# A four-layer graph kernel on one Trainium2 core: the last batch's first products of each quarter come together behind the other batches'

## The chip, the cores and the metric

The kernel runs on one core of a Trainium2 chip. The core has five engines that run side by side, each through its own list of instructions in order: TensorE (PE in the profile; its weight loads are shown apart as PEld), VectorE (DVE), ScalarE (ACT), GpSimd (POOL) and SyncE (SP, which here only issues DMAs). They meet through semaphores. The metric is the device time of one execution in microseconds (us), the median of several.

## The reference: what is computed

The input is a batch of 16 graphs with the same adjacency matrix `adj` of 1024 x 1024 nodes and 256 features for each node. There are four layers. Layer 0 scores every pair of nodes and sums over the scored edges:

```python
hidden = relu(pre_u[:, :, None, :] + pre_v[:, None, :, :] + b1)
S = sigmoid(einsum('buvk,ko->buvo', hidden, W2)[..., 0] + b2[0])
a_t = einsum('buv,bud->bvd', S * A_a, h_t)                 # the scored sums
m_t = einsum('uv,bud->bvd', A_m, h_t) * h_t
z_t = beta1 * h_t + beta2 * (a_t @ Wa + ba) + beta3 * (m_t @ Wm + bm)
```

Layer 1 sends messages along `adj` and adds a relu of them. Layers 2 and 3 are attention layers: a projection, a softmax over `leaky_relu(f1_i + f1_j) + adj`, a weighted sum, and the input added.

The change is in the scored sums of layer 0, the line with `a_t`. The kernel multiplies `h_t` by `Wa` first (this product is called `hw`), so the stage computes, for each batch, `hw` transposed times `S * A_a`: a contraction over the 1024 source nodes `u`.

## The kernel before, in words

**Sparse scores, dense products.** `adj` is sparse. The scores are worked out for listed neighbours only, by `score_steps` (L717): GpSimd gathers a row of features for each listed slot (L708), VectorE adds and multiplies (L825, L827), ScalarE sums four batches' results (L831, four instructions for one step), and GpSimd scatters the finished scores into a dense array in HBM, `dense_d` (L713). This work runs beside everything else: a helper (`Side.along`, L888) takes a step from it whenever the main work has advanced by so many us (`PACE`).

**Groups.** The 16 batches are worked on in four groups of four (`GB = 4`). For each group, `with_edges` (L1120) computes the scored sums, and then `group_layers` (L1355) does the other layers. While group g is in its layers, the scores of group g+1 are made. In group 3 no score work is left.

**A quarter.** `with_edges` cuts the 1024 target nodes into four quarters of 256 columns. A quarter holds all eight PSUM banks: one for each of the four batches and two halves of the features, `acc[i][eh]`. Its contraction runs over eight tiles of 128 source nodes, `ut`. For each tile:

- SP loads `gd`, the dense scores of the tile for four batches, 512 KB (`load_gd`, L904; four buffers);
- ScalarE copies it into `gc`, with the batches side by side instead of interleaved (L1129; two buffers, `gc_pool`, L702);
- TensorE makes eight products (L131, the line of the helper `product`), for batch 0 to 3 and both halves: `hw[i]` of the tile times `gc` of that batch, summed in the bank of `acc[i][eh]`.

After the eighth tile, VectorE evicts the eight banks in the order of the batches, adds a bias and what is already in `z` (L1152), and the next quarter takes the same banks. There are 16 quarters in the program, 64 products in each.

**What sets the order.** A scheduling layer decides each engine's list and puts in the waits for data and buffers. So a `gc` copy waits until the products that read its buffer two tiles before are done, until its `gd` has landed, and behind all that stands before it on ScalarE. On top of that the kernel paces itself: `paced(ins, n)` (L123) makes an instruction wait for the product that was issued n products earlier in the program's text. A `gc` copy is paced 16 products back, a `gd` load 24, a score step's L825 six. The list `recent`, which is counted in, follows the order in which `product` is called.

**Around the stage.** Before a group's first quarter the banks belong to the last attention layer of the group before: ScalarE copies them (L1325), VectorE finishes (L1326, L1328), and ScalarE issues the output's DMAs (L1002). After the last quarter come the layer-1 products.

Of the kernel before, what the change touches and what calls it, by code (L numbers as in the profile page):

```python
# [17 lines left out]
P = 128  # L18

GB = 4  # L20
# [50 lines left out]
def gnn_stack_kernel(  # L71
# [29 lines left out]
    NT = N // P  # L101
# [4 lines left out]
    QN = HN // 2  # L106
# [6 lines left out]
    def bank():  # L113
        return psum[-1].tile([P, HN], F32, tag="bank", name="bank")
# [8 lines left out]
    def paced(ins, back=6):  # L123


        if recent:
            after(tc, ins, [recent[max(0, len(recent) - back)]], mybir.DependencyClass.Sync, "keeps pace")
        return ins

    def product(*args, **kw):  # L130
        recent.append(nc.tensor.matmul(*args, **kw))  # L131
        del recent[:-BACK]
        return recent[-1]
# [554 lines left out]
    with tc.If(listed > 0) as arm:  # L688
        with ExitStack() as stack:
# [214 lines left out]
            def load_gd(g, v, ut, **pace):  # L904
                view = dense[g % BUFS][:DUMP].rearrange("(t p v) b -> t p v b", p=P, v=N)
                gd = gd_pool.tile([P, QN, GB], F32, tag="gd", name="gd")
                ins = nc.sync.dma_start(gd, view[ut][:, v * QN : (v + 1) * QN, :])
                put[g].before(paced(ins, **pace))
                return gd
# [207 lines left out]
            def exponential(jt):  # L1117
                paced(nc.scalar.activation(ea[:, jt, :], ea[:, jt, :], AF.Exp), 16)

            def with_edges(g, hw, z):  # L1120

                doing[0] = "edges"
                for v in range(N // QN):
                    cols = slice(v * QN, (v + 1) * QN)
                    acc = [[bank() for _ in range(DH)] for _ in range(GB)]
                    for ut in range(NT):
                        gd = first_gd.pop(0) if first_gd else load_gd(g, v, ut, back=BACK)
                        gc = gc_pool.tile([P, GB, QN], F32, tag="gc", name="gc")
                        paced(nc.scalar.activation(gc, gd.rearrange("p n i -> p i n"), AF.Copy), 16)  # L1129
                        for i in range(GB):  # L1130
                            for eh in range(DH):
                                product(
                                    acc[i][eh][:, :QN], hw[i][:, ut, eh * P : (eh + 1) * P], gc[:, i, :],
                                    start=ut == 0, stop=ut == NT - 1,
                                )
                        if z_loads and ut % 2 == 0:
                            load, i = z_loads.pop(0)
                            paced(load(i), 12)
                        if (to_load or to_exp) and ut % 2 and v:
                            if v > 1 and to_exp:  # L1140
                                exponential(to_exp.pop(0))
                            if to_load:
                                jt = to_load.pop(0)
                                paced(nc.sync.dma_start(ea[:, jt, :], adjT_d[jt]), 16)
                                to_exp.append(jt)
                        yield 3.4 if g or v else 1
                    if v == N // QN - 1:
                        while to_exp:
                            exponential(to_exp.pop(0))
                    for i in range(GB):  # L1150
                        for eh in range(DH):
                            nc.vector.scalar_tensor_tensor(  # L1152
                                z[i][:, eh, cols], acc[i][eh][:, :QN], zbias[:, eh : eh + 1], z[i][:, eh, cols],
                                ALU.add, ALU.add,
                            )
# [264 lines left out]
            for g in range(NGR):  # L1420
                hw, z = loaded.pop(0)
                while g not in finished:
                    next(side.steps)
                side.along(with_edges(g, hw, z))
                if g < NGR - 1:
                    side.along(group_layers(g, z))
                else:
                    for _ in far_ahead(z[2:], pair_layers(g * GB, z[:2], layer_one(z[:2]))):
                        pass
                    for _ in pair_layers(g * GB + 2, z[2:], from_lists(z[2:], msg)):  # L1430
                        pass
# [131 lines left out]
```

## Time and profile before

| | us |
|---|---|
| median of three runs | 3143.56 (3133.77 to 3150.67) |
| the profiled execution, its own time | 3123.2 |
| its span, first to last instruction | 3121.5 |
| TensorE busy | 3074.8 |
| VectorE, ScalarE, GpSimd busy | 2352.6, 1945.1, 1878.9 |
| scored sums, groups 0 to 3 | 121.4, 116.6, 120.0, 110.8 |

The mean granted clock of TensorE is 0.998 of full speed. All durations below are from the one profiled execution, whose time lies 20 us under the median of the runs.

How to read the rows: a row of a timeline has the start (us from the span's start), the duration, the engine, the line of the source, the operation, what it writes `<-` what it reads, the shape, and in brackets how long the engine stood idle before it and what ended that. Rows of equal instructions in sequence are merged (`x2`). A row of waits has who waited, `<-` for what, then the total in us, how many times, and the longest. An fp32 product stands in the profile as two matmul records. Idle time of an engine counts only if the end of the run hangs on it.

### The profile page before, as it was taken

To read this page: it belongs to the slowest core of one execution; us is meant where nothing else is said; L and a number is where in the kernel's file an instruction comes from. 1 tells how busy PE (TensorE), PEld (TensorE's weight loads), DVE (VectorE), ACT (ScalarE), POOL (GpSimd) and SP (SyncE) were. 2 spreads that over 40 slices of the span, in tenths; PEclk is the share of its full clock that TensorE was granted. 3 is DMA by queue.
4 is the path that set the end of the run, shared out by engine and by line. 5 is a ranking of instruction groups with operands and counts; after the bars stand their busy time and mean duration, and the time that the engine had idled before them with its cause. 6 is when DMAs were issued, how large, how long until landed. Compare 5 with 4: busy or idle time off the path is not lost. (4 is left out here: it accounts for less than half of the span.)

```text
span 3121.5 us, 39024 instructions
## 1 busy us (share of the span) xinstructions
PE 3074.8 (99%) x11954; PEld 2179.2 (70%) x11954; DVE 2352.6 (75%) x3183; ACT 1945.1 (62%) x6520; POOL 1878.9 (60%) x1483
## 2 busy tenths in 40 slices
PE   9999999999999999999999999999999999999999
PEld 5544555545547756888875688888568888858888
DVE  7887777768774678999667899966789982157844
ACT  3345565656667876787887677788667764414242
POOL 1156787777664577777666776766777770076600
PEclk9999999999999999999999999999999999999999
DMA  9998898888889776568877665887765565485500
GB/s 321 331 331 310 270 313 260 273 242 253 254 290 331 229 214 202 156 185 285 285 233 207 209 165 171 266 284 232 219 206 164 159 207 166 132 262 156 164 2 28
DMA packets 288420, 699.96 MB, mean 224 GB/s; under 512 B 46141, under 2 KB 141178, under 8 KB 281034
## 3 DMA queue, kind: packets, MB, share of 16 engines
q0 software_dynamic: 128224, 387.80, 42.5%
q1 hardware_dynamic: 132538, 258.46, 23.7%
q10 hardware_dynamic: 27440, 51.13, 4.3%
q8 instruction: 96, 1.57, 0.2%
q14 instruction: 122, 1.00, 0.1%
HBM read 565.83 MB, written 131.41 MB: 223 GB/s over the span
## 5 line engine op out<-in xcount | busy, mean ns | idle before, releaser
L831 ACT ACTIVATE z<-z 128x256 f32<-128x256 f32 x2432 | 979.0, 406 | 574.1 <-DVE z L827 549.0
L825 DVE TENSOR_TENSOR z<-z,u 128x1024 f32<-128x1024 f32 x608 | 738.9, 1220 | 374.8 <-PE bank L131 262.4
L131 PE MATMUL bank<-feats,m 128*128 128x257 f32 x4096 | 909.0, 380 | 0.7 <-ACT st L1325 0.5
L708 POOL DMA_INDIRECT z<-v_d,slot_v x512 | 662.2, 1293 | 376.0 <-ACT z L831 208.1
L131 PEld LDWEIGHTS bank<-feats,m 128*128 128x128 f32 x4096 | 769.4, 190 | 111.2 <-ACT st L1325 1.3
L713 POOL DMA_INDIRECT dense_d<-gt,slot_at x512 | 674.5, 1317 | 184.4 <-issue 130.3
L827 DVE SCALAR_TENSOR_TENSOR z<-z,w2r 128x1024 f32<-128x1024 f32 x608 | 737.3, 1219 | 9.0
L131 PE MATMUL bank<-gc,hw 128*128 128x256 f32 x2048 | 451.8, 382 | 15.6 <-ACT gc L1129 10.5
L831 ACT ACTIVATION_READ_ACCUMULATOR z<-z 128x1 f32 x2432 | 461.6, 190 | 0.0
L131 PE MATMUL bank<-adj_sb,h 128*128 128x512 f32 x1024 | 442.3, 592 | 3.3 <-ACT st L333 2.0
L131 PEld LDWEIGHTS bank<-gc,hw 128*128 128x128 f32 x2048 | 386.6, 190 | 80.2 <-ACT gc L1129 20.7
L1099 DVE SCALAR_TENSOR_TENSOR m<-rho,tau,adj_sb 128x512 f32<-128x512 f32 x512 | 375.8, 742 | 65.6 <-PE bank L131 62.7
L131 PE MATMUL bank<-adjT_in,y 128*128 128x512 f32 (+1 forms) x960 | 403.4, 581 | 6.0 <-DMA adjT_in<-adjT_d 5.9
L131 PEld LDWEIGHTS bank<-adj_sb,h 128*128 128x128 f32 x1024 | 194.3, 190 | 242.7 <-issue 237.5
L131 PEld LDWEIGHTS bank<-adjT_in,y 128*128 128x128 f32 x960 | 182.0, 191 | 221.0 <-issue 203.8
L131 PE MATMUL bank<-w,hT 128*128 128x512 f32 (+1 forms) x1024 | 334.9, 487 | 0.0
L1129 ACT ACTIVATE gc<-gd 128x1024 f32<-128x1024 f32 x128 | 264.7, 2069 | 88.4 <-PE bank L131 74.9
L131 PEld LDWEIGHTS bank<-w,hT 128*128 128x128 f32 x1024 | 194.8, 191 | 141.5 <-issue 118.4
L131 PE MATMUL bank<-g_wT,z 128*128 128x257 f32 x1024 | 231.4, 380 | 1.6 <-ACT st L1325 1.1
L131 PEld LDWEIGHTS bank<-g_wT,z 128*128 128x128 f32 x1024 | 191.8, 190 | 33.2 <-issue 3.1
L708 POOL DMA_INDIRECT z<-v_d,x_node x96 | 124.2, 1294 | 128.6 <-ACT z L831 96.6
L1152 DVE SCALAR_TENSOR_TENSOR z<-bank,zbias,z 128x256 f32<-128x256 f32 x128 | 54.6, 480 | 111.7 <-PE bank L131 111.4
(168 smaller groups left out, 2379.4 us busy)
## 6 DMA issues: line engine op xcount, KB each, us to landing
gd<-dense_d SPq DMA_DIRECT2D x128, 512.0 KB
dense_d<-zero ACTq DMA_DIRECT2D x64, 512.0 KB
adjT_in<-adjT_d SPq DMA_DIRECT2D x112, 256.0 KB
h<-in_x_dram SPq DMA_DIRECT2D x19, 1024.0 KB
u_d<-st SPq DMA_DIRECT2D x64, 256.0 KB
v_d<-st SPq DMA_DIRECT2D x64, 256.0 KB
hw_d<-st SPq DMA_DIRECT2D x64, 256.0 KB
u<-u_d POOLq DMA_DIRECT2D x32, 512.0 KB
```

The source lines that it names most:

```text
L131: recent.append(nc.tensor.matmul(*args, **kw))
L708: return nc.gpsimd.indirect_dma_start(out=dst, out_offset=None, in_=src[:], in_offset=bass.IndirectOffsetOnAxis(ap=at, axis=0), **how,)
L713: return nc.gpsimd.indirect_dma_start(out=dst[:], out_offset=bass.IndirectOffsetOnAxis(ap=at, axis=0), in_=src, in_offset=None,)
L825: paced(nc.vector.tensor_tensor(z, z, u, ALU.add))
L827: nc.vector.scalar_tensor_tensor(zk, zk, 0.0, w2r[:, None, :].to_broadcast([P, GB, D]), ALU.max, ALU.mult)
L831: nc.scalar.activation(zk[:, c, :], zk[:, c, :], AF.Copy, accum_out=s[:, k, c : c + 1])
L1099: nc.vector.scalar_tensor_tensor(m, r[:, cols], ta[:, kt : kt + 1], ea[:, kt, cols], ALU.max, ALU.mult)
L1129: paced(nc.scalar.activation(gc, gd.rearrange("p n i -> p i n"), AF.Copy), 16)
L1152: nc.vector.scalar_tensor_tensor(z[i][:, eh, cols], acc[i][eh][:, :QN], zbias[:, eh : eh + 1], z[i][:, eh, cols], ALU.add, ALU.add,)
```

## The change

Within a quarter, the products of the last batch (`i = GB - 1`, banks 6 and 7) for tiles 0 and 1 are held back. Tile 0 issues the six products of batches 0 to 2. Tile 1 issues its own six, and then the held four: the last batch's two of tile 0, and its two of tile 1. From tile 2 on the order is as before. No product, copy or eviction is added or left out; the buffers' numbers stay.

```diff
                     acc = [[bank() for _ in range(DH)] for _ in range(GB)]
+                    held_back = []
                     for ut in range(NT):
                         gd = first_gd.pop(0) if first_gd else load_gd(g, v, ut, back=BACK)
                         gc = gc_pool.tile([P, GB, QN], F32, tag="gc", name="gc")
                         paced(nc.scalar.activation(gc, gd.rearrange("p n i -> p i n"), AF.Copy), 16)
-                        for i in range(GB):
+
+                        turns = [(ut, gc, i) for i in range(GB - 1 if ut < 2 else GB)]
+                        if ut < 2:
+                            held_back.append((ut, gc, GB - 1))
+                        if ut == 1:
+                            turns += held_back
+                        for kt, scores, i in turns:
                             for eh in range(DH):
                                 product(
-                                    acc[i][eh][:, :QN], hw[i][:, ut, eh * P : (eh + 1) * P], gc[:, i, :],
-                                    start=ut == 0, stop=ut == NT - 1,
+                                    acc[i][eh][:, :QN], hw[i][:, kt, eh * P : (eh + 1) * P], scores[:, i, :],
+                                    start=kt == 0, stop=kt == NT - 1,
                                 )
```

In the changed kernel the lines behind the change stand seven lower: the `gc` copy is L1130, the evictions L1159, and L1325, L1326 and L1328 become L1332, L1333 and L1335.

## The prediction

> **What bounds the kernel now.** I read the page first, then TensorE's waits, then the stage that the change touches, by its four stretches, and last the ScalarE rows inside it.
>
> ```profile
> span 3121.5 us, 39024 instructions
> PE 3074.8 (99%) x11954; PEld 2179.2 (70%) x11954; DVE 2352.6 (75%) x3183; ACT 1945.1 (62%) x6520; POOL 1878.9 (60%) x1483
> ...
> PE bank L131 <- ACT gc L1129: 10.5, 12, 2.2
> ```
>
> TensorE is busy for all but 46.7 us of the span, so a pause put into it lengthens the run, unless a pause already there becomes shorter. The longest named wait is for the `gc` copies of the stage in question (10.5 us in 12 waits). The next view cuts that stage into its four groups (window, its length, then busy time by engine, granted clock, DMA share, GB/s):
>
> ```profile
> 942.00:1063.40 121.40, 114.31 (x517) 96.61 (x516) 64.01 (x80) 103.78 (x210) 52.51 (x45) 1.00 0.88 305
> 1495.40:1612.00 116.60, 113.75 (x517) 96.69 (x516) 75.70 (x96) 106.03 (x246) 69.37 (x58) 1.00 0.84 270
> 2045.30:2165.30 120.00, 114.35 (x516) 97.84 (x515) 77.65 (x92) 105.00 (x243) 74.73 (x62) 0.99 0.84 271
> 2598.00:2708.80 110.80, 110.80 (x516) 97.55 (x515) 15.02 (x37) 61.79 (x31) 0.53 (x1) 1.00 0.47 150
> ```
>
> Group 3 has no score work beside it, and TensorE never pauses: 512 matmul records in 110.8 us are 0.216 us each. An fp32 product is two records, so 0.432 us; a tile of 8 products 3.45; a quarter 27.7. Groups 0 to 2 take 10.6, 5.8 and 9.2 us more (25.6 in all): there ScalarE is busy for some 105 us. Call the copies of a quarter gc0 to gc7. Group 3, around a quarter's start:
>
> ```profile
> 2622.47 2.08 ACT L1129 ACTIVATE gc<-gd 128x1024 f32<-128x1024 f32 x1 [1.40 <-PE bank L131]
> 2625.92 2.06 ACT L1129 ACTIVATE gc<-gd 128x1024 f32<-128x1024 f32 x1 [1.38 <-PE bank L131]
> 2629.37 2.05 ACT L1129 ACTIVATE gc<-gd 128x1024 f32<-128x1024 f32 x1 [1.39 <-PE bank L131]
> 2632.83 2.05 ACT L1129 ACTIVATE gc<-gd 128x1024 f32<-128x1024 f32 x1 [1.40 <-PE bank L131]
> ```
>
> These are gc0 to gc3. There are two `gc` tiles, so gc2 cannot start before the products of gc0 are done: ScalarE idles 1.4 us until TensorE frees a tile, copies for 2.05, and is done ahead of need. gc2 starts at 2629.37, 0.25 after the record that follows gc0's last product (2629.12). It ends at 2631.42; TensorE wants it when tile 1 is done, 0.25 before gc3's start: 2632.58. Slack 1.16 us.
>
> **The change, part by part.** *Work.* The same 64 products per quarter, copies and evictions: 0 us. In the order of the changed program, every quarter runs six products of tile 0, six of tile 1, then the last batch's two of tile 0 as the 13th and 14th, and its two of tile 1. (In groups 1 and 2, whose starts were already permuted, one or two products differ.)
>
> *What it gives: banks 6 and 7 are wanted later.* They are the last that VectorE evicts from the quarter before. The gain is at most what TensorE waits for these evictions: the source view of L1152 gives 0.4 us in two waits of weight loads over the whole run. I take 0.
>
> *What it costs: gc2.* gc0 is now read until the 14th product instead of the 8th, so gc2 starts 6 x 0.432 = 2.59 us later. The slack covers 1.16 less the hand-over from copy to matmul, 0.05 (a copy that ends at 958.18 is followed at 958.23, rows below). The pause is 2.59 - 1.11 = 1.48, and the record after a pause steps 0.32 instead of 0.216: about 1.6 us for each quarter. gc3 then runs straight behind gc2, ends 2.05 after it, 1.4 before it is wanted; the usual spacing is back. Group 3: 4 x 1.6 = 6.4.
>
> *gc1* is wanted after six products (2.59 us into the quarter, was 3.45). In group 3 it ends at 0.25 + 2.06 = 2.31: no wait. Where score work stands ahead of it it ends later: at 3.54 in three quarters (a pause of 1.0), at 3.04 and 2.73 in two (0.5 and 0.2); this also pushes the 14th product.
>
> *Score work queued beside gc2.* In the changed order of eight quarters, the four L831 of one score step (1.6 us; a score batch, below) have moved from behind gc2 to ahead of it. They fill time that ScalarE would have idled, or overrun it. Second quarter of group 1, before:
>
> ```profile
> 1527.53 2.10 ACT L1129 ACTIVATE gc<-gd 128x1024 f32<-128x1024 f32 x1 [0.26 <-ACT gc L1129]
> ...
> 1531.13 2.11 ACT L1129 ACTIVATE gc<-gd 128x1024 f32<-128x1024 f32 x1
> ...
> 1531.20 1.23 DVE L827 SCALAR_TENSOR_TENSOR z<-z,w2r 128x1024 f32<-128x1024 f32 x1
> ```
>
> The quarter starts at 1527.32. Now gc1 ends at 1529.6, a first batch at 1531.2; the second waits for the L827 that ends at 1532.43 and ends at 1534.1; the 14th product is done at 1533.36. So gc2 runs 1534.2 to 1536.3 and tile 2 starts at 1536.35 instead of 1534.33: +2.0. The same working, from each quarter's own rows: first quarters of groups 0 and 1 below; the other three of group 0 +1.0, +0.85, +1.9; of group 1 +2.0, +2.0, +2.3; of group 2 +2.2, +1.4, +1.9. Where it is under 1.5 (between 0.4 and 1.5 for the first of them), a later pause of the old quarter (up to 1.3 us, for a copy or a `gd` load) shrinks by the rest.
>
> *First quarters.* Group 0: tile 2 is 1.5 late, but TensorE already pauses at tiles 4 and 5 for `gd`; the load for tile 4 is paced behind the ninth product, whose time stays, so it lands as before. Between 0 and 1.6, as the load for tile 5 is issued that much later or lands with the backlog: I take the middle, 0.8. Group 1: gc2 starts 7.5 us in already, behind score work and an output DMA, past the new release (6.8): 0. Group 2 is worse. The score step after tile 0 is paced six products back, now the quarter's first product instead of its third, and in the changed VectorE order its L825 comes ahead of the pair of L1328 that frees the sixth bank:
>
> ```profile
> 2048.14 0.87 DVE L1328 SCALAR_TENSOR_TENSOR st<-st,share,bank 128x256 f32<-128x256 f32 x2
> 2052.09 1.23 DVE L825 TENSOR_TENSOR z<-z,u 128x1024 f32<-128x1024 f32 x1 [3.08 <-PE bank L131]
> ```
>
> That L825 waits for its gather, which lands at 2052.00. The pair then runs at 2053.3 to 2054.2 and TensorE, after seven products from 2045.31, stands from 2048.3 to 2054.3. Such a pause costs clock as well: the granted clock after the present one, 2.80 us at 2055.71, was
>
> ```profile
> 2055.70:2059.00 3.30, 3.29 (x8) 0.54 0.90 294
> 2059.00:2080.00 21.00, 21.00 (x98) 0.99 0.91 304
> ```
>
> so the next four products take 0.85 each, the 14th is done at 2059.1, gc2 ends at 2061.4 and tile 2 starts then instead of 2059.04: +2.4.
>
> *Queues.* GpSimd issues one `u` gather two scatters earlier, in group 0; SP moves an `adjT_in` load past a store and the first `gd`; both stay ahead of their users: 0. The `gd` loads from tile 5 on are paced 24 products back and shift with TensorE.
>
> Sum: 6.4 + 3.75 + 6.3 + 5.5 + 0.8 + 0 + 2.4 = 25.15, say 25 us. On the profiled execution (3123.2 us) that is 3148; that execution lies 20 us below the median of the three runs, 3143.56, so against the median I forecast 3169, +0.8%.
>
> **A rule against the trace.** A pause of TensorE that ended in full clock is this one:
>
> ```profile
> 956.16 2.02 ACT L1129 ACTIVATE gc<-gd 128x1024 f32<-128x1024 f32 x1 [3.27 <-PE bank L131]
> 958.23 3.72 PE L131 MATMUL bank<-gc,hw 128*128 128x256 f32 x16 [2.18 <-ACT gc L1129]
> ```
>
> 2.18 us idle cost no clock here, 2.80 did. My pauses of 1.3 to 2.1 idle lie below both, the one of 6 us above. A tripped clock adds 1.7 us (eight records at 0.427 instead of 0.216). Pauses with one score batch more, 1.6 longer (B below), would be of 2.9 to 3.7 and trip it by the row: in eight quarters 13.6 us more. The Trainium skill, "TensorE: Matmul & The Clock Gate", Part 1, says that the clock halves after an idle window of about 3.4 us, counted by a free-running clock; by it most of these pauses would cost no clock, and the sum there would lack those 13.6. For my forecast row and rule give the same, and the measured 2.80 decides where they part.
>
> **The rivals.** *A, swallowed.* Groups 0 to 2 already lose 25.6 us to late copies and loads; if the new pauses only stand in their place, group 3's 6.4 remain, with what exceeds them: about +10, 3153. For: ScalarE is busy for 105 of 120 us there. Against: 15 of the lost us lie in the three first quarters, and in five of the nine others the old pauses after tile 2 sum to under 0.8.
>
> *B, larger.* A second score batch ahead of gc2 in eight quarters (8 x 1.6 = 13), or the clock tripped in as many (13.6): +38, 3182; both, +52. For: batches wait for VectorE (549 us of ScalarE's waits). Against: the order has one more, not two.
>
> *C, the other side: late banks are the real loss at a quarter's start.* From quarter start to tile 2, the 16 quarters lose 11.2 us against 6.91 each, 9.5 of them at the starts of groups 1 and 2, where banks come from L1325 and L1328. If all came back and gc2 were not late, 3132. It decides only where gc2's delay stays under 0.7 us a quarter; against it stand group 3's rows. By this alone the gain stays within 0.5%; run spread would have to add to it.
>
> *D, no change.* A scheduler could restore the old order; the changed program shows the move in all 16 quarters.
>
> **How the numbers follow.** Forecast (+17 to +33) 0.58, A 0.14, B 0.18, C 0.09, D 0.01. The bounds: A's +10 less half of the runs' spread (8) gives 3146, B's +38 with the same gives 3190; I give 3148 to 3190, and 3160 to 3177 for the forecast alone. Within 0.5% (15.7 us) is about what a measurement of this kernel cannot tell from no change. Slower takes the forecast, B and a fifth of A: 0.79. Same: the rest of A, half of C, D: 0.16. Faster: the other half of C, with the spread: 0.05.
>
> **What would show it.** In group 3: gc2 starts 6.3 us into each quarter instead of 3.7, ScalarE idles 4.0 us before it and 0 before gc3, TensorE pauses once a quarter at tile 2 for about 1.3 us of shown idle, and the stretch is 117 us instead of 110.8. In all, `gc` waits go from 10.5 us to some 25 to 30. At the start of group 2, a pause of about 6 us and a half clock after it. Wrong would be: gc2 starting at 3.7 all the same; tile 2 late but the stretches of groups 0 to 2 unchanged (A); pauses over 3 us at tile 2 (B).

## The result and the profile after

| | before | after |
|---|---|---|
| median of six runs each, same chip | 3142.06 (3132.87 to 3150.67) | 3165.61 (3154.68 to 3171.13) |
| ratio of the two, 95% interval | | 1.0079 (1.006 to 1.0098) |
| the profiled execution, its own time | 3123.2 | 3169.96 |

The medians differ by 23.5 us (a ratio of 1.0075); by the interval the change costs between 19 and 31. The page of the changed kernel, with the lines that answer to those of before (a group of instructions has busy time and mean ns of one, then the idle time just before them and what ended most of it):

```profile
span 3168.2 us, 39029 instructions
...
PE 3081.3 (97%) x11954; PEld 2179.1 (69%) x11954; DVE 2352.2 (74%) x3183; ACT 1946.2 (61%) x6520; POOL 1876.7 (59%) x1483
...
L131 PE MATMUL bank<-gc,hw 128*128 128x256 f32 x2048 | 455.2, 382 | 39.1 <-ACT gc L1130 29.4
...
L1130 ACT ACTIVATE gc<-gd 128x1024 f32<-128x1024 f32 x128 | 262.7, 2061 | 109.7 <-PE bank L131 75.3
```

The engines do the same work: ScalarE is busy for 1946.2 us (1945.1 before), the 128 copies take 2061 ns each. TensorE's idle time ahead of the stage's products is what grew: 39.1 us, of which 29.4 are waits for `gc`. Before, the same row had 15.6 and 10.5:

```profile
L131 PE MATMUL bank<-gc,hw 128*128 128x256 f32 x2048 | 451.8, 382 | 15.6 <-ACT gc L1129 10.5
```

TensorE's waits after the change (total in us, times, longest):

```profile
PE bank L131 <- ACT gc L1130: 29.4, 26, 1.7
...
PE bank L131 <- DVE st L1335: 6.2, 1, 6.2
```

The second line is a single pause, at the start of group 2. The stage by its four groups (window, its length, then busy time by engine, granted clock, DMA share, GB/s):

```profile
951.70:1077.80 126.10, 114.56 (x515) 96.19 (x514) 63.70 (x79) 103.58 (x210) 50.95 (x44) 1.00 0.87 294
1509.90:1632.50 122.60, 114.28 (x516) 96.14 (x515) 75.54 (x96) 106.11 (x246) 66.59 (x58) 1.00 0.81 257
2066.60:2196.00 129.40, 115.28 (x516) 97.50 (x515) 77.80 (x92) 104.83 (x243) 72.03 (x62) 0.97 0.78 250
2637.40:2754.40 117.00, 111.87 (x517) 97.22 (x515) 15.02 (x37) 61.29 (x31) 0.53 (x1) 1.00 0.42 142
```

They were 121.4, 116.6, 120.0 and 110.8, so the four take 26.3 us more. In group 3, which has no score work, the reason is in plain sight. A quarter's start there, with ScalarE's copies and TensorE's products (a row has the start, the duration, and in brackets the idle time before it and what ended that):

```profile
2659.70 13.98 PE L131 MATMUL bank<-gc,hw 128*128 128x256 f32 x64
...
2663.41 2.08 ACT L1130 ACTIVATE gc<-gd 128x1024 f32<-128x1024 f32 x1 [1.40 <-PE bank L131]
2666.86 2.07 ACT L1130 ACTIVATE gc<-gd 128x1024 f32<-128x1024 f32 x1 [1.38 <-PE bank L131]
2672.90 3.95 ACT L1130 ACTIVATE gc<-gd 128x1024 f32<-128x1024 f32 x2 [3.98 <-PE bank L131]
...
2674.97 7.39 PE L131 MATMUL bank<-gc,hw 128*128 128x256 f32 x33 [1.29 <-ACT gc L1130]
```

The quarter starts at 2666.61 (this moment and the lengths of single quarters below are read from the matmul records one by one). gc1 starts 0.25 us later. gc2 (the first of the two merged in the row at 2672.90) starts 6.29 us into the quarter instead of 3.7, since its buffer is now read until the 14th product; ScalarE stands idle for 3.98 us before it, and gc3 follows without a gap. TensorE pauses 1.29 us for it, once in every quarter.

The profiled pair differs by 46.7 us, though, and the medians by 23.5. Of the 46.7, the four groups hold 26.9, counted from first to last record of each. The rest lies outside: 9.7 us ahead of the first changed product, 8.6 in the layers of group 2, and so on. The profiled execution of the changed kernel lies near the top of its runs, the other under all of the six of the kernel before. A second profile of each kernel (below) shows what these are.

### The profile page after: what moved, and what is told of

Its sections match the earlier page's. It is cut to its first block, busy times and chain, and to the rows that moved or that the text cites. A ratio compares the mean times of both kernels' runs of the same rounds, so it can differ in the third digit from the quotient of the medians.

```text
span 3168.2 us, 39029 instructions
## 1 busy us (share of the span) xinstructions
PE 3081.3 (97%) x11954; PEld 2179.1 (69%) x11954; DVE 2352.2 (74%) x3183; ACT 1946.2 (61%) x6520; POOL 1876.7 (59%) x1483
## 5 line engine op out<-in xcount | busy, mean ns | idle before, releaser
L825 DVE TENSOR_TENSOR z<-z,u 128x1024 f32<-128x1024 f32 x608 | 738.3, 1219 | 410.2 <-PE bank L131 250.4
L713 POOL DMA_INDIRECT dense_d<-gt,slot_at x512 | 663.6, 1296 | 188.3 <-issue 137.3
L131 PE MATMUL bank<-gc,hw 128*128 128x256 f32 x2048 | 455.2, 382 | 39.1 <-ACT gc L1130 29.4
L1130 ACT ACTIVATE gc<-gd 128x1024 f32<-128x1024 f32 x128 | 262.7, 2061 | 109.7 <-PE bank L131 75.3
L1159 DVE SCALAR_TENSOR_TENSOR z<-bank,zbias,z 128x256 f32<-128x256 f32 x128 | 54.6, 479 | 117.4 <-PE bank L131 117.2
```

The lines of the kernel that those rows point to most:

```text
L713: return nc.gpsimd.indirect_dma_start(out=dst[:], out_offset=bass.IndirectOffsetOnAxis(ap=at, axis=0), in_=src, in_offset=None,)
L825: paced(nc.vector.tensor_tensor(z, z, u, ALU.add))
L1159: nc.vector.scalar_tensor_tensor(z[i][:, eh, cols], acc[i][eh][:, :QN], zbias[:, eh : eh + 1], z[i][:, eh, cols], ALU.add, ALU.add,)
```

## The experiments

Four chips took part; a ratio is always against runs of the kernel before on the same chip. This table puts the profiles side by side. "13 quarters" is the sum of all quarters but the first ones of groups 0, 1 and 2, which stand alone in the last column. A quarter is counted from the start of its first record to the end of its last; a pause between two quarters is in neither (2.8 us behind the 30.32 of the first split, at most 0.9 elsewhere).

| kernel | ratio (95%) | `gc` waits | group 3 | 13 quarters | first quarters of groups 0, 1, 2 |
|---|---|---|---|---|---|
| before | 1 | 10.5 | 110.67 | 369.8 | 31.94, 31.95, 34.77 |
| before, second profile | | 18.7 | 110.67 | 370.9 | 32.84, 37.53, 40.51 |
| after | 1.0079 (1.006 to 1.0098) | 29.4 | 116.87 | 391.5 | 32.81, 32.08, 38.80 |
| after, second profile | | 28.8 | 116.87 | 391.0 | 33.02, 31.70, 41.38 |
| after, copy split 3+1 | 0.9968 (0.9951 to 0.9984) | 10.8 | 110.67 | 369.3 | 31.70, 30.60, 30.32 |
| before, copy split 3+1 | 0.9976 (0.996 to 0.9991) | 8.7 | 110.67 | 370.0 | 32.58, 30.18, 29.32 |
| the same, another chip | 1.0000 (0.9987 to 1.0013) | 8.4 | 110.67 | 369.4 | 31.30, 30.18, 34.36 |
| before, copy split 2+2 | 0.9978 (0.996 to 0.9996) | 6.9 | 110.67 | 370.4 | 30.73, 32.69, 32.70 |
| tile 0's pair after one batch | 0.9994 (0.9977 to 1.0012) | 16.9 | 110.67 | 374.5 | 31.89, 31.61, 38.29 |
| tile 0's pair after two batches | 1.0034 (1.0017 to 1.0051) | 25.0 | 113.51 | 384.0 | 36.33, 31.46, 41.07 |
| first quarters left alone | 1.0071 (1.0046 to 1.0096) | 30.5 | 115.36 | 389.9 | 31.84, 38.63, 31.92 |
| pace restored | 1.0089 (1.0065 to 1.0113) | 34.6 | 116.91 | 392.2 | 32.97, 38.53, 33.87 |
| pace restored, second profile | | 34.3 | 116.89 | 390.7 | 32.41, 37.78, 36.91 |
| before, with the pace alone | 1.0008 (0.9996 to 1.002) | 8.5 | 110.67 | 369.6 | 32.65, 30.81, 31.08 |

### The buffer's release: the copy split, in the changed kernel and in the one before

The theory: the loss is the late release of gc0's buffer. If the last batch, whose products are late, has a tile of its own, the other three batches' buffer is free early again. The order of the products stays.

```diff
-                        gc = gc_pool.tile([P, GB, QN], F32, tag="gc", name="gc")
-                        paced(nc.scalar.activation(gc, gd.rearrange("p n i -> p i n"), AF.Copy), 16)
+                        gc = gc_pool.tile([P, GB - 1, QN], F32, tag="gc", name="gc")
+                        gl = gc_pool.tile([P, 1, QN], F32, tag="gl", name="gl")
+                        by_batch = gd.rearrange("p n i -> p i n")
+                        paced(nc.scalar.activation(gc, by_batch[:, : GB - 1, :], AF.Copy), 16)
+                        paced(nc.scalar.activation(gl, by_batch[:, GB - 1 :, :], AF.Copy), 16)
...
```

In the changed kernel:

> The changed kernel with each gc tile split in two tiles of two buffers each: batches 0 to 2, and the last batch alone (two copies for a tile instead of one, 256 more ScalarE instructions' halves in all). The held products then keep only the small tile. Release theory (the copy of tile 2 waits for the held products of tile 0): the large copy of tile 2 is free after the sixth product, so the pause at tile 2 goes; group 3's stage takes 110.7 us instead of the changed kernel's 116.9, groups 0 and 1 lose 4 to 6 us each, and only the 6 us pause at the start of group 2 stays: about the split control plus 4 to 7 us, 3146 to 3152. Rival, order (TensorE itself pays for the new order of products or banks): group 3 stays near 116.9 and the time near 3165.

In the kernel before, as the control for what the split does by itself:

> The kernel before with the same split of the copies, as a control for what the split costs by itself: one more ScalarE start for each of 128 tiles, some 0.2 to 0.4 us each. Where ScalarE idles (group 3) it is hidden: 110.7 us. In groups 0 to 2 it may add 0 to 3 us each. Total within 0 to +8 us of the kernel before (3142 to 3150), under both theories.

Group 3 of the changed kernel with the split copy (window as above, then some of its copies):

```profile
2603.70:2714.50 110.80, 110.80 (x516) 97.58 (x515) 15.02 (x36) 64.69 (x61) 0.53 (x1) 1.00 0.49 150
```

```profile
2634.26 1.59 ACT L1132 ACTIVATE gc<-gd 128x768 f32<-128x768 f32 x1 [1.30 <-issue]
2636.85 1.59 ACT L1132 ACTIVATE gc<-gd 128x768 f32<-128x768 f32 x1 [1.00 <-PE bank L131]
2638.34 1.20 ACT L1133 ACTIVATE gl<-gd 128x256 f32<-128x256 f32 x2
```

All 110.80 us are busy again, with the products in the changed order. The quarter shown starts at 2631.42; the larger part of gc2 starts at 2634.26, 2.84 us into it instead of 6.29. The 13 quarters take 369.3 us, as in the kernel before. So the order of the products costs nothing by itself; what costs is that one late reader holds a tile of four batches. The Trainium skill, "Perfetto Trace Analysis", Optimizing Scalar/DVE Operations, says that where ScalarE is not saturated but causes bubbles on another engine, breaking up its instructions may let work complete sooner. The split does that here, mainly because it divides the tile and so lets the next copy start sooner. The rows show its price: 1601 + 658 ns for the two parts instead of 2061 for one, some 25 us of ScalarE over the run, of which the 13 quarters show nothing.

Both split kernels are 10 us faster than the kernel before on this chip, which I had not expected. Nor is the changed kernel with the split 4 to 7 us above its control, as forecast: the medians are 3129.89 and 3129.91, and the pause at the start of group 2, forecast at 6 us, was 1.59 in its profile. I come back to it with the third split.

### The dose: tile 0's pair a little earlier

If the release is the cause, the cost must follow it in steps: with tile 0's held products after the first batch of tile 1 the buffer is free two products late, which the slack covers; after the second batch, four products late.

```diff
                         if ut == 1:
-                            turns += held_back
+                            turns = turns[:1] + held_back[:1] + turns[1:] + held_back[1:]
```

> The changed kernel with tile 0's two held products issued after the first batch of tile 1 (as 9th and 10th product instead of 13th and 14th); tile 1's two stay last. Release theory: gc2 is released 2 products later than before, 0.86 us, less than the 1.11 us of slack, so group 3 shows no pause at tile 2 (110.7 us), groups 0 and 1 stand within 2 to 3 us of before, and the pause at the start of group 2 (VectorE's order) stays: 3146 to 3152. Rival, order: the products still change places, so each quarter still pays some 1.5 us: about 3165, group 3 near 117.

The same with `turns[:2]` and `turns[2:]`:

> The same with tile 0's two held products after the second batch of tile 1 (11th and 12th). Release theory: gc2 is released 4 products later, 1.73 us, less 1.11 of slack: a pause of 0.62 us and 0.10 for the record after it, so 0.7 us a quarter; group 3 takes 113.6 us, between 110.7 and 116.9, and the total is about 3153 to 3159. Rival, order: as the changed kernel, 3165, group 3 near 117.

Group 3 after one batch (TensorE, then ScalarE's gc2 and gc3):

```profile
2631.65 13.54 PE L131 MATMUL bank<-gc,hw 128*128 128x256 f32 x62
...
2636.86 2.05 ACT L1130 ACTIVATE gc<-gd 128x1024 f32<-128x1024 f32 x1 [2.25 <-PE bank L131]
2639.45 2.06 ACT L1130 ACTIVATE gc<-gd 128x1024 f32<-128x1024 f32 x1 [0.54 <-PE bank L131]
```

and after two:

```profile
2663.65 3.97 ACT L1130 ACTIVATE gc<-gd 128x1024 f32<-128x1024 f32 x2 [3.12 <-PE bank L131]
...
2665.74 6.53 PE L131 MATMUL bank<-gc,hw 128*128 128x256 f32 x29 [0.45 <-ACT gc L1130]
```

ScalarE's idle time before gc2 goes 1.4, 2.25, 3.12, 3.98 for a release none, two, four and six products late: 0.86 a step, two products. TensorE's pause goes 0, 0, 0.45, 1.29: nothing up to the slack, then one for one. Group 3 takes 110.67, 110.67, 113.51, 116.87. The ratios follow: 0.9994, 1.0034, 1.0079. Only the total of the first missed: 3 us under the kernel before on this chip, where the expectation's 3146 to 3152 was 4 to 10 above the 3142 known then.

### Which quarters: the first ones left alone

```diff
-                        turns = [(ut, gc, i) for i in range(GB - 1 if ut < 2 else GB)]
-                        if ut < 2:
+                        turns = [(ut, gc, i) for i in range(GB - 1 if v and ut < 2 else GB)]
+                        if v and ut < 2:
```

> The changed kernel, but a group's first quarter keeps the order of before (products are held back in quarters 1 to 3 alone). Release theory: the twelve other quarters keep their pause (1.1 to 2.3 us each), the four first ones lose theirs: group 3 takes 110.7 + 3 x 1.56 = 115.4 us, and the first quarters of groups 0, 1 and 2 return to about 31.9, 32.0 and 34.8 us; total 5 to 8 us under the changed kernel, 3158 to 3161. If VectorE's order at the start of group 2 were not tied to the move, that quarter would stay near 38.8.

Group 3, its first quarter and its second (window and length, then busy time by engine):

```profile
2620.50:2648.40 27.90, 27.90 (x132) 24.59 (x131) 4.48 (x12) 14.66 (x8) 0.00 (x0) 1.00 0.57 189
2648.40:2677.70 29.30, 28.00 (x131) 24.32 (x130) 3.62 (x10) 16.30 (x9) 0.00 (x0) 1.00 0.41 144
```

The cost is local: the quarter with the old order takes 27.8 us and never pauses, the next one pauses 1.3. Group 2's first quarter fell to 31.92. But group 1's took 38.63, although its products stand in the old order. That was open here. The 5 to 8 us that the whole run should have gained do not show either: 1.0071 (1.0046 to 1.0096) against 1.0079.

### The start of group 2: the pace of the score step

The prediction put a pause of 6 us down to one L825 that the pace moves ahead of a pair of evictions. It was there (PE and DVE rows of the changed kernel):

```profile
2066.65 3.19 PE L131 MATMUL bank<-gc,hw 128*128 128x256 f32 x14
...
2073.85 1.23 DVE L825 TENSOR_TENSOR z<-z,u 128x1024 f32<-128x1024 f32 x1 [4.07 <-DMA z<-v_d,slot_v]
2075.00 0.87 DVE L1335 SCALAR_TENSOR_TENSOR st<-st,share,bank 128x256 f32<-128x256 f32 x2
...
2076.01 5.63 PE L131 MATMUL bank<-gc,hw 128*128 128x256 f32 x18 [6.17 <-DVE st L1335]
```

The gather landed 7.2 us into the quarter; TensorE stood for 6.17 us behind the pair, and then ran 18 records in 5.63 us, with the clock halved for a part of them. Two kernels take this apart. In the first, the changed order keeps the old pace: two entries more are counted after tile 0, and taken out again at tile 1.

```diff
+                        if ut == 1:
+                            del recent[-2:]
                         turns = [(ut, gc, i) for i in range(GB - 1 if ut < 2 else GB)]
...
+                        if ut == 0:
+                            recent.extend(recent[-1:] * 2)
```

> The changed kernel with the pace of the score step after tile 0 put back: the list that the pace counts in is padded by two, so the step's L825 waits for the third product of the quarter instead of the first. In the built order L825 then stands behind the pair of evictions again at the start of groups 1 and 2; the products are all held back as in the changed kernel. Theory (the extra pause at the start of group 2 comes from L825 ahead of the pair on VectorE, not from the held products): the pause of 6.2 us there falls to about 1.5 and 3 us at the two banks that come late, tile 2 starts some 13.2 us into the quarter instead of 16.3, and the quarter takes 35 to 36 us instead of 38.8; the pauses at tile 2 of the other quarters stay, group 3 takes 116.9; total 2 to 4 us under the changed kernel, 3162. Rival (the pause there belongs to the held products and the release of gc): the quarter stays near 38.8.

The pair ran first and the 6 us pause was gone:

```profile
2068.34 2.32 PE L131 MATMUL bank<-gc,hw 128*128 128x256 f32 x10
2072.74 5.38 PE L131 MATMUL bank<-gc,hw 128*128 128x256 f32 x16 [2.08 <-DVE st L1339]
```

The quarter took 33.87 us, a little under the expectation. Yet the ratio, 1.0089, is no lower than the changed kernel's, and the first quarter of group 1 was again at 38.53. In the second, the kernel before keeps its products and gets the new pace alone. On VectorE this moves one thing at two places: at the starts of groups 1 and 2, an L825 goes ahead of a pair that frees a bank.

```diff
+                        if ut == 1:
+                            recent.extend(skipped)
                         for i in range(GB):
...
+                        if ut == 0:
+                            skipped = recent[-2:]
+                            del recent[-2:]
```

> The kernel before, its products in their old order; only the score step behind tile 0 of each quarter is paced two products further back, as the change does it. On VectorE this moves one thing at two places: at the starts of groups 1 and 2, an L825 now stands ahead of a pair that frees a bank, as in the changed kernel. Theory (the pause at the sixth bank of group 2 comes from that L825, which waits for its gather): a pause at the 11th or 15th record of group 2's first quarter of 2.5 to 7 us, followed by half clock, quarter 37 to 43 us instead of 34.8 and 40.5; all other quarters as before, group 3 110.67, gc waits 9 to 19 us; time 1.000 to 1.003 of the kernel before. Rival (the pause belongs to the late release of gc, or to nothing but the execution): no pause above 2.1 us at the sixth bank, quarter 32 to 41, ratio 0.999 to 1.001. A ratio over 1.004 would say that the pace costs more than the order of the products.

```profile
2042.66 3.19 PE L131 MATMUL bank<-gc,hw 128*128 128x256 f32 x14
...
2045.62 1.23 DVE L825 TENSOR_TENSOR z<-z,u 128x1024 f32<-128x1024 f32 x1 [0.48 <-DMA z<-v_d,slot_v]
2046.76 0.87 DVE L1333 SCALAR_TENSOR_TENSOR st<-st,share,bank 128x256 f32<-128x256 f32 x2
...
2047.78 4.12 PE L131 MATMUL bank<-gc,hw 128*128 128x256 f32 x18 [1.93 <-DVE st L1333]
```

My expectation of a pause of 2.5 to 7 us missed. The chain is the same, gather, L825, pair, TensorE, but the gather landed 3 us into the quarter instead of 7.2, and TensorE stood for 1.93 us. The quarter took 31.08 us, and the ratio says that the pace alone costs between -1 and 6 us. By the expectation's own signs this run fits the rival as well.

All the profiles together decide it. In six of the fourteen the L825 stands ahead of the pair (after and its second profile, after with the split, both dose runs, the pace alone). It starts 7.20, 6.51, 2.62, 3.12, 6.35 and 2.96 us into the quarter, and TensorE's pause ahead of the 15th record is 6.17, 5.47, 1.59, 2.09, 5.32 and 1.93 us: 1.03 or 1.04 less, each time. In the other eight the pair runs first; they pause 0.8 to 2.1 us ahead of the 11th record, where the six do not pause. So the order on VectorE does make TensorE wait for a gather, and the length of that pause is set by when the gather lands. That changes from execution to execution. What the whole quarter loses by it is not shown, as the old order has pauses of its own there.

### What comes back: second profiles of three kernels

The kernel before, unchanged:

> The kernel before, profiled once more. What belongs to the kernel should come back within 1 us: group 3 at 110.7 us, its quarters at 27.79, tile 2 at 6.91 us into a clean quarter, and about 9 to 13 us in waits for gc copies. If a first quarter of group 1 or 2 that took 38 us in other runs (a late landing of a gather or of a gd load) is a matter of the execution, it may turn up here too, in a kernel without the change; if it belongs to the changed order, the first quarters of groups 1 and 2 stay at 30 to 35 us.

The changed kernel, unchanged:

> The changed kernel, profiled once more. My theory: group 3 is again 116.9 us, a clean quarter 29.35 with tile 2 at 8.3 us, and the quarters 2 to 4 of groups 0 to 2 again 29.9 to 31.2; those nine lie 1.1 to 2.3 above the kernel before. The first quarter of group 2 has again a pause before the sixth bank is evicted, but of a length set by when the gather lands: between 1.5 and 7 us, quarter between 33 and 39. The rival, that the excess of the profiled pair outside the stage (9.7 us ahead of the first changed product and 8.6 in the layers of group 2) belongs to the change: then the first changed product starts again at 951.8 +-1 us from the start and the layers behind group 2 take again 8 us more than in the kernel before. By my theory these move by several us from run to run.

The changed kernel with the old pace, once more:

> The changed kernel with the score step's pace restored in the quarters' first tiles, profiled once more. Group 3 again 116.9 us, the first quarter of group 2 again at 33 to 35 us with the evicting pair ahead of the L825. Open is the first quarter of group 1, which took 38.5 us in the profile of this kernel: if that belongs to this kernel's order it comes back within 1 us; if it is a late landing of a gd load in that execution, it is 30 to 33 us here.

The first profile of these three shows the kernel before at the start of group 1:

```profile
1527.29 2.01 ACT L1129 ACTIVATE gc<-gd 128x1024 f32<-128x1024 f32 x1 [5.02 <-remote]
...
1529.35 15.97 PE L131 MATMUL bank<-gc,hw 128*128 128x256 f32 x64 [6.47 <-ACT gc L1129]
```

So the first quarter of 37 to 39 us in group 1 needs no part of the change. It is there in the kernel before, where gc2 waited 5.02 us. `remote` in the row means that the profile found no instruction that ended just when the wait did. It was not the load of `gd`: ScalarE's wait for that load's semaphore was over at 1521.49, after 0.02 us. What gc2 then waited for was TensorE's semaphore. TensorE's last product ahead of the pause ends at 1522.88 by its record, but its semaphore was still counted up at 1522.92, 1524.40, 1525.86 and 1527.26, and gc2 started 0.03 us after the last of these. Why the signals came so late stays open. Four of the fourteen profiles have such a quarter, with the same sequence in the trace: this one, the kernel with its first quarters left alone, and both with the old pace. With the old pace it came back within 1 us (37.78 after 38.53), which the expectation had named as the sign of that order, so that order may still make it more frequent; neither profile of the changed kernel itself has it. Group 2's first quarter, too, takes 34.77 and 40.51 us in the kernel before. Nothing about the first quarters can be learned from one profile of each.

Some expectations missed: the `gc` waits of the kernel before were 18.7 us instead of 9 to 13 (6.5 of them in this one pause), the first quarter of group 2 took 41.38 us in the changed kernel (33 to 39 expected) and 36.91 with the old pace (33 to 35). Of the nine quarters with score work one, the second of group 0, was no longer than before in the second pair.

What lies outside the stage changes as well: 2654.1 and 2678.0 us in the two profiles of the kernel before, 2673.9 and 2660.5 in those of the changed one. The 19.8 us by which the first pair differs outside the stage turn into 17.5 the other way round in the second. The first changed product started at 944.1 us instead of 951.8, and the layers of group 2 took 0.3 us more than before instead of 8.6. So these differences can't be put down to the change.

What comes back to within 1.2 us are the 13 other quarters: 369.8 and 370.9 before, 391.5 and 391.0 after. The means differ by 20.9 us. That is nearly the whole of the 23.5 between the medians; the rest lies within the interval.

### The split copy as a change of its own

The copy split in two halves of two batches, in the old order:

```diff
...
+                        gc = gc_pool.tile([P, 2, QN], F32, tag="gc", name="gc")
+                        gl = gc_pool.tile([P, 2, QN], F32, tag="gl", name="gl")
+                        paced(nc.scalar.activation(gc, by_batch[:, :2, :], AF.Copy), 16)
+                        paced(nc.scalar.activation(gl, by_batch[:, 2:, :], AF.Copy), 16)
...
```

> The order of the kernel before, with each gc copy in two halves of two batches and two buffers for each half. Theory (what decides is how long a gc buffer is held, and so how early the next copy may start): the first half may start after 4 of 8 products of the tile two before instead of after 8, 1.73 us earlier, and takes about 1.15 us instead of 2.07 (between the 0.66 of one batch and the 1.60 of three), so its slack at tile 2 grows from 1.1 to about 3.7 us; waits for gc copies under 9 us, group 3 110.7, tile 2 at 6.91, groups 0 to 2 at 112 to 119, time 0.9955 to 0.998 of the kernel before, like the split in three and one (0.9976). Rival: ScalarE's extra time counts (two halves 2.3 us instead of 2.07, 128 times, some 30 us of ScalarE): then 1.000 to 1.004.

0.9978, with group 3 at 110.67: as expected (group 0, at 120.5 us, lay above the 112 to 119). On another chip, where the kernel before takes 3123.43 us instead of 3139.93, the 3+1 split was run again:

> The kernel before with its gc copy split into three batches and one, once more, to see whether its gain holds and whether its first quarters stay short. Theory (a buffer released earlier takes a late copy off TensorE's path): ratio 0.996 to 0.999 again, first quarters of groups 1 and 2 again 28 to 34 us, where the kernel before took 32 and 35 in one profile, 37.5 and 40.5 in another. Rival (those 38 us are late gd loads and gathers, which the split does not touch): a first quarter of 37 to 41 us turns up here too.

There it gained nothing: 1.0000. The rival's quarter of 37 to 41 us did not turn up, and the theory's 28 to 34 were just missed by 34.36. No split loses in these runs: the split in three and one gains 10 us on one chip and nothing on another, the split in halves 6 on a third. The 13 quarters are the same with and without it (369.3 to 370.9), so its gain is not in them. It may be in the first quarters of groups 1 and 2, which took 29 to 34 us in all four profiles with a split, and up to 40.5 in the kernel before. On the chip without a gain, the kernel before with the pace alone had short ones too (30.81 and 31.08), which would fit. That is an argument from five profiles, and nothing here settles it.

## Why the prediction held, and which of its terms did not

The forecast was 3169 us and +25; the medians gave 3165.6 and +23.5. For the 13 quarters it had 22.0, and the profiles gave 20.9. Its other 3.2 us, for the first quarters of groups 0 to 2, are not shown: the profiles' means differ there by +0.5, -2.9 and +2.5. So a part of the closeness of +25 to +23.5 is luck. Its steps, one by one:

*The clean quarter.* Forecast: gc2 starts at 6.3, ScalarE idles 4.0 before it and 0 before gc3, TensorE pauses 1.3, 1.6 us a quarter, 117 for the group. Measured: 6.29, 3.98, 0, 1.29, 1.51 to 1.56 a quarter, 117.0. The dose runs confirm the slack as well: they bend between two and four products.

*The quarters with score work.* Means of the two pairs of profiles, for the second to fourth quarters: group 0 +0.6, +1.6, +1.3 (forecast +1.0, +0.85, +1.9); group 1 +2.0, +2.2, +1.8 (+2.0, +2.0, +2.3); group 2 +1.7, +1.2, +2.3 (+2.2, +1.4, +1.9). Sums 3.6, 6.0 and 5.2 against 3.75, 6.3 and 5.5. The single terms of group 0 were off by up to 0.8 us. For its third quarter I let the old pause shrink. In fact the old pause at the fifth tile, a step of 1.17 us, now stands at the seventh with the same 1.17. In the fourth, more of the old pauses went than I had taken. The two errors nearly cancel.

*gc1 wanted earlier.* In the first profile, pauses of 0.6 to 0.9 us ahead of the 13th record, behind six products, in five of the nine quarters (steps of 0.8 to 1.1 less the usual 0.216). The forecast had five as well, three of 1.0 and two of 0.5 and 0.2; they came out more even.

*The start of group 2.* The mechanism was right: L825 ahead of the pair, 6.17 us of pause, half clock after it. The term, +2.4, is the one that I would take back. The two pairs gave +4.0 and +0.9; that their mean comes to 2.5 is luck. It was worked out from the gather's landing in one execution, 6.7 us into the quarter, as if it were fixed. The landing was at 7.2 in the changed kernel and at 3 in the kernel with the pace alone, whose quarter, 31.08, was even below before's 34.77 and 40.51. The same holds for the 0 at the start of group 1, where +0.1 in one pair and -5.8 in the other say nothing. For the first quarters of groups 1 and 2 I should have given a spread of some 6 us each, not terms.

*Evictions: a gain of 0.* The clean quarter's 1.51 to 1.56 leaves room for at most 0.1 a quarter.

*The rivals.* A (swallowed): the nine quarters with score work would have had to stay the same; they took 14.7 us more. B (larger): no pause of the changed kernel at tile 2 exceeded 2 us, as one more batch would have made it. C (late banks are the real loss) needed a gc2 that is under 0.7 us late; tile 2 began 1.2 us later or more in every quarter of the first pair but one, the first of group 1. D (no change) is out: the trace has the products in the new order.

*The clock.* I had placed the limit between 2.18 us of idle time, which cost no clock, and 2.80, which did. The forecast's pauses stayed free, but the limit is not one for a pause: where the pause falls counts too, as the last section shows.

## What to carry to other kernels

A tile is free when its last reader is done, so moving one reader back holds the whole tile, and with two buffers the producer's slack is what pays. Work out that slack from a stretch with no other work (here 1.1 us, 2.6 products). Here every product by which the last reader moved cost its full time beyond the slack, in each repetition. Where readers must come apart, give the late part a tile of its own. And profile a kernel twice before a term is taken from a single event, like the landing of one gather: the sums over many quarters came back to 1.2 us, the first quarters only to 6.

## What the runs showed of the hardware

*The clock does not go by the length of a pause alone.* In the kernel before, 2.18 us of idle time were followed by records at full clock (16 records in 3.72 us). In the kernel with the old pace, 2.08 us were followed by 16 records in 5.38 us (row above), of which seven took 0.43 instead of 0.216. The second profile of the changed kernel has both kinds of pause:

```profile
2067.14 6.21 PE L131 MATMUL bank<-gc,hw 128*128 128x256 f32 x18 [5.47 <-DVE st L1335]
...
2087.54 12.75 PE L131 MATMUL bank<-gc,hw 128*128 128x256 f32 x50 [2.09 <-ACT gc L1130]
```

After 2.09 us, seven of the next records took 0.43, the first of them the fifth after the pause; at full clock the 50 would have taken about 11.1 (16 take 3.72). The pauses at tile 2, up to 1.7 us of idle time, were never followed by a half clock in the changed kernel's two profiles.

The trace's record of the granted clock tells the two apart. In all fourteen profiles a stretch at half clock (but for the one at the end of each run) lasts 3.41 us, or two or three times that, and within a profile all of them start on one grid of 3.413 us. Here are the windows of that grid around two pauses, the 2.18 us of the kernel before and then the 2.09 us above (the window, its length, TensorE's busy time first, and the granted clock third from the end):

```profile
953.43:956.84 3.41, 2.62 (x13) 1.96 (x11) 0.00 (x0) 0.68 (x1) 1.70 (x2) 1.00 1.03 415
956.84:960.25 3.41, 2.02 (x9) 1.82 (x10) 0.00 (x0) 1.33 (x1) 0.00 (x0) 1.00 1.03 407
```

```profile
2085.02:2088.43 3.41, 1.32 (x7) 0.84 (x6) 3.34 (x4) 3.00 (x6) 0.00 (x0) 1.00 0.83 294
2088.43:2091.84 3.41, 3.41 (x10) 2.70 (x9) 2.41 (x3) 2.90 (x6) 2.10 (x2) 0.50 0.70 208
```

The 2.18 us fall into two windows, 0.8 and 1.4 us; the 2.09 us fall into one, and the next window runs at half clock. Of all the windows at full clock in the stage, in fourteen profiles, the 21 with 2.06 us or more of idle time were followed by half clock, and none of the 1964 with 1.85 or less was. Outside the stage the border is less sharp: 1.86 us tripped the clock once, 1.98 did not once. The Trainium skill, "TensorE: Matmul & The Clock Gate", Part 1, says that the clock is set by a free-running window of about 3.4 us. The grid agrees with that. The page has the clock halve after an idle window; here some 2 us of idle time in one window were enough, and a window at half clock costs up to 1.7 us (half of 3.41).

*A copy in two parts costs little.* The copy of four interleaved batches takes 2061 to 2071 ns, of three 1600 to 1605, of two 1131 to 1135, of one 657 to 662. Each batch of 256 columns adds about 0.47 us, and a further instruction about 0.2. The rows of a group, before with 3+1:

```profile
L1131 ACT ACTIVATE gc<-gd 128x768 f32<-128x768 f32 x128 | 205.5, 1605 | 74.5 <-issue 32.9 <-PE bank L131 20.7 <-DMA gd<-dense_d 19.2
...
L1132 ACT ACTIVATE gl<-gd 128x256 f32<-128x256 f32 x128 | 84.8, 662 | 0.0
```

*From chip to chip the time moves as much as by the change.* The kernel before took 3138.97, 3139.93, 3145.69 and 3123.43 us (medians) on the four chips of the experiments. That is a spread of 0.7%, about what the change costs, so only ratios on one chip were compared. Each chip was used in one session, so a chip and its moment are not told apart.
